# Layer 3's output tiles: odd tiles stored through ScalarE's DMA queue instead of GpSimd's, and the general path's stores off GpSimd's queue too

## The chip, the cores and the metric

One Trainium2 chip, one of its cores. The metric is device time in microseconds (us) of one execution, the median of a few runs. Engines are named as in the profile: PE (TensorE), DVE (VectorE), ACT (ScalarE), POOL (GpSimd) and SP (SyncE, which here only issues DMAs).

## What is computed

Four graph layers on 2708 nodes with 256 features, each followed by a residual and a layer norm. The adjacency matrix is dense in storage. Cut to what matters here:

```
x = LN(x + adj @ (x * w0))                         # layer 0
x = LN(x + attention(x, adj > 0))                  # layer 1, 4 heads
x = LN(x + signed_attention_and_GRUs(x, adj))      # layer 2, 3 heads, uses adj > 0 and adj < 0
h = adj @ (x @ neigh_W.T) / (adj.sum(1) + 1)       # layer 3
x = LN(x + concat(x, h) @ lin_W.T)
```

The output has 2708 rows of 256 floats: 22 tiles of 128 rows, the last of 20.

## The kernel before

**The main path.** The kernel streams the adjacency matrix from HBM again in every layer and multiplies tiles of it on PE. In layers 2 and 3 the nodes are cut into two halves and each half into three units of 512, 512 and 330 columns; a seven-product scheme (`seven`, L309) forms the products, with the operand sums on DVE (L296 to L299). The last part of the program is layer 3: for each of the three units, eleven chunks of the matrix are loaded into three rotating buffers `p` by SP (`load_pairs`, L256), one chunk feeding 14 matmul records of L309.

**Finishing rows.** What a unit has accumulated is gathered (L317 to L327: one copy on ACT, four adds on DVE), and then a generator, `rows3`, finishes one row tile at a time: two transposes on PE (L1172), a scaled add on DVE (L1173), the moments on DVE (L162 to L166) with the power -1/2 on POOL (L167), one small multiply on DVE (L1177), the normalization on ACT (L1178), and the store of the tile to the output (L1179). Rows of unit 0 (tiles 0 to 3 and 11 to 13) are finished between the matmuls of unit 1, those of unit 1 (4 to 7 and 14 to 17) between the matmuls of unit 2, and those of unit 2 (8 to 10 and 18 to 21) after the last matmul, at the end of the program: `between()` takes one step of the generators after products 2 and 5 of each chunk. Even tiles are stored through SP's queue, odd ones through POOL's.

**The order of work.** Each engine takes its instructions in the order in which the program was built; an engine's DMAs wait in that same order. A framework adds the semaphores: each DMA takes one of eight semaphores of its kind in turn (one set of eight for SP's and ACT's DMAs together, one for POOL's), and a DMA waits until the one that had its semaphore before it has landed.

**The general path.** Layers 2 and 3 in the main path are valid for a matrix without negative entries. A flag `signed` is computed in layer 1, and at the end of the program stands a branch (L1425): where the flag is set, `layer2_signed()` and `layer3()` compute both layers again. With the inputs here it isn't set, and the body is skipped. Two stores to DRAM stand in that body: `layer2_end` (L219, 22 stores of `y3_d`) and `layer3` (L1225, 22 stores of the output). On the skipping side of the branch the framework puts instructions that bring each semaphore to the count that it would have had after the body, so that what follows can wait for one number whichever side ran. For the semaphores of SP's, ACT's and the engines' own these are single semaphore updates; for those of POOL's DMAs it is one POOL instruction that the trace calls INC_SWDGE_SEM. After it, under L1468 (the end of the program's context), SP waits for all semaphores, every engine executes a DRAIN and they meet in a barrier; POOL is the one that collects the others and releases them, and then clears the semaphores.

Of the kernel before, what the change touches and what calls it, by code (L numbers as in the profile page):

```python
# [19 lines left out]
P = 128  # L20
# [7 lines left out]
def kernel(  # L28
# [24 lines left out]
    nc = tc.nc  # L53
# [27 lines left out]
    def sz(i):  # L81
        return min(P, N - i * P)
# [19 lines left out]
    def pool(name, bufs=1, **kw):  # L102
        return tc.tile_pool(name=name, bufs=bufs, reuse_waits="tile", **kw)
# [34 lines left out]
    y3_d = [dram.tile([sz(t), F], F32, name=f"y3_{t}") for t in range(NT)]  # L138
# [20 lines left out]
    def moments(src, n):  # L159

        bst = small.tile([P, 6], F32, tag="bn_st", name="bn_st")
        nc.vector.bn_stats(bst[:n], src[:n])  # L162
        mv = small.tile([P, 2], F32, tag="bn_mv", name="bn_mv", bufs=12)
        nc.vector.bn_aggr(mv[:n], bst[:n])
        rstd = small.tile([P, 1], F32, tag="bn_rs", name="bn_rs", bufs=12)
        nc.vector.tensor_scalar(rstd[:n], mv[:n, 1:2], EPS, None, ALU.add)  # L166
        nc.gpsimd.tensor_tensor(rstd[:n], rstd[:n], neg_half[:n], ALU.pow)  # L167
        return mv[:n, 0:1], rstd[:n]

    def layernorm(dst, src, n):  # L170

        mean, rs = moments(src, n)
        nc.vector.tensor_scalar(dst[:n], src[:n], mean, rs, ALU.subtract, ALU.mult)

    def transposed(ps, pool, src, n, tag):

        pt = ps.tile([P, 4, P], F32, tag="tr", name="tr")
        for f in range(FC):
            nc.tensor.transpose(pt[:, f, :n], src[:n, f * P : (f + 1) * P], ident[:n, :n])
        dst = pool.tile([P, FC, P], F32, tag=tag, name=tag)  # L180
        nc.scalar.copy(dst[:, :, :n], pt[:, :FC, :n])
        return dst
# [9 lines left out]
    def load_strip(pool, t):  # L192
        s = pool.tile([P, NT, P], F32, tag="strip", name="strip", bufs=2)
        nc.sync.dma_start(s, adj_t[t])
        return s
# [5 lines left out]
    def strip_matmul(acc, s, n, rhs):  # L201
        for c in range(NT):
            nc.tensor.matmul(acc, s[:, c, :n], rhs(c), start=(c == 0), stop=(c == NT - 1))  # L203
# [6 lines left out]
    def layer2_end(ps, pool, lwn, t, y):  # L210

        n = sz(t)
        xt = transposed(ps, pool, y, n, "xt")
        pz = ps.tile([P, 2 * F], F32, tag="pz", name="pz")
        for f in range(FC):
            nc.tensor.matmul(pz[:n], xt[:, f, :n], lwn[:, f, :], start=(f == 0), stop=(f == FC - 1))
        nc.scalar.copy(h3[t][:n], pz[:n, F:])
        nc.vector.tensor_tensor(y[:n], y[:n], pz[:n, :F], ALU.add)
        nc.gpsimd.dma_start(y3_d[t], y[:n])  # L219

    def gru_columns(pool, b, bih, bhh):

# [90 lines left out]
    def gathered(pool, m, w, wide, tag, bufs=1):  # L313

        m1, m26, m75, m43 = m
        m1s = pool.tile([P, wide], F32, tag="m1s", name="m1s", bufs=2)
        nc.scalar.copy(m1s[:, :w], m1[:, :w])  # L317
        y = pool.tile([P, FC, 2, wide], F32, tag=tag, name=tag, bufs=bufs)
        yq = y.rearrange("p f h w -> p (f h) w")[:, :, :w]
        nc.vector.tensor_tensor(  # L320
            yq[:, 0::3], m1s[:, None, :w].to_broadcast([P, 2, w]), m26[:, :, :w], ALU.add
        )
        nc.vector.tensor_tensor(
            yq[:, 1:3], yq[:, 3:4].to_broadcast([P, 2, w]), m75[:, :, :w], ALU.add
        )
        nc.vector.tensor_tensor(yq[:, 3], yq[:, 1], m75[:, 1, :w], ALU.add)
        return y, nc.vector.tensor_tensor(yq[:, 1:3], yq[:, 1:3], m43[:, :, :w], ALU.add)  # L327
# [57 lines left out]
    if True:  # L385
# [13 lines left out]
        if True:  # L399
# [162 lines left out]
            if True:  # L562
# [276 lines left out]
                for lo in range(0, NT, 4):  # L839
# [3 lines left out]
                    for t in range(lo, hi):  # L843
                        n = sz(t)
# [80 lines left out]
    with (  # L925
# [10 lines left out]
        def bank():  # L936
            return banks.tile([P, W], F32, tag="bank", name="bank")
# [132 lines left out]
        def by_tiles(lo, w, src, ends):  # L1070

            tiles, at = [], 0
            for t, c0, c1 in pieces(lo, w):
                got = src(at, c1 - c0)
                at += c1 - c0
                if c1 - c0 < sz(t):
                    first = t not in ends
                    if first:
                        ends[t] = nleft.tile([P, FC, P], F32, tag=f"yt{t}", name=f"yt{t}")
                    nc.gpsimd.tensor_copy(ends[t][:, :, c0:c1], got)  # L1080
                    if first:
                        continue
                    got = ends[t]
                tiles.append((t, got))
            return tiles
# [40 lines left out]
        for u, (_, w) in enumerate(units):  # L1126
            est = [nleft.tile([P, FC, W], F32, tag="est", name="est", bufs=3) for h in range(2)]
            for k in range(K):
# [23 lines left out]
                y, summed = gathered(nleft, m, w, W, "yk")  # L1152
# [6 lines left out]
        def complete(u):  # L1159

            return [t for t in by_end if ends_at[t] == u]

        def rows3(u, y, o8):

            a, w = units[u]
            for h in range(2):
                for t, src in by_tiles(h * NH + a, w, lambda at, n: y[:, :, h, at : at + n], shared3):
                    n = sz(t)
                    o = o8[:, complete(u).index(t)]
                    pt = bank()  # L1170
                    for f in range(FC):
                        nc.tensor.transpose(pt[:n, f * P : (f + 1) * P], src[:, f, :n], ident)  # L1172
                    nc.vector.scalar_tensor_tensor(  # L1173
                        o[:n], pt[:n, :F], rdeg[:n, t : t + 1], o[:n], ALU.mult, ALU.add
                    )
                    mean, rs = moments(o, n)
                    nc.vector.scalar_tensor_tensor(mean, mean, -1.0, rs, ALU.mult, ALU.mult)  # L1177
                    nc.scalar.activation(o[:n], o[:n], AF.Identity, scale=rs, bias=mean)  # L1178
                    (nc.gpsimd if t % 2 else nc.sync).dma_start(out[t * P : t * P + n, :], o[:n])  # L1179
                    yield  # L1180


# [2 lines left out]
        for u, (_, w) in enumerate(units):  # L1185
            m = accumulators()
            for i, c in enumerate(lead):
                early3 = u == 0 and max(ends_at[2 * c], ends_at[2 * c + 1]) + 1 < len(units)
                if u == 0:
                    if not early3:  # L1190
                        while urgent or later:
                            between()
                    hq[c] = quarter_sums(xqp, h3, c, "hq")
                pa = nright.tile([P, 2, 2, W], F32, tag="p", name="p", bufs=3)
                load_pairs(units, u, c, pa)
                if i == MH - 3:
                    o8 = (nleft if u % 2 else hold).tile([P, 4 * W // F, F], F32, tag="blk", name="o8")
                    for j, t in enumerate(complete(u)):
                        nc.gpsimd.dma_start(o8[: sz(t), j], y3_d[t])
                with tc.issue_after(summed.ins):  # L1200
                    seven(nright, m, pa, h3, hq[c], c, w, i == 0, i == MH - 1, range(7) if early3 else (2, 5))
            y, summed = gathered(nleft, m, w, W, "yk")
            later.append(rows3(u, y, o8))
# [8 lines left out]
    def layer3():  # L1212
        with pool("l3", 2, side="right") as l3, pool("ps_3", 3, space=PSUM) as ps_3:
            for t in range(NT):
                n = sz(t)
                s = load_strip(l3, t)
                o = l3.tile([P, F], F32, tag="o", name="o")
                nc.sync.dma_start(o[:n], y3_d[t])
                acc = ps_3.tile([P, 512], F32, tag="acc", name="acc")
                strip_matmul(acc[:n, :F], s, n, lambda c: h3[c])  # L1220
                nc.vector.scalar_tensor_tensor(
                    o[:n], acc[:n, :F], rdeg[:n, t : t + 1], o[:n], ALU.mult, ALU.add
                )
                layernorm(o, o, n)
                nc.gpsimd.dma_start(out[t * P : t * P + n, :], o[:n])  # L1225

    def layer2_signed():
        TG = 4
# [127 lines left out]
        with tc.tile_pool(name="l2b", bufs=1) as l2b:  # L1356
# [5 lines left out]
            for t in range(NT):  # L1362
# [56 lines left out]
                )  # L1419
                layernorm(y, y, n)  # L1420
                layer2_end(ps_t, work, lwn, t, y)
        stack.close()


    with tc.If(nc.values_load(signed[0:1, 0:1], min_val=0, max_val=1) > 0):  # L1425
        layer2_signed()
        layer3()
# [44 lines left out]
```

## Time and profile before

| | us |
|---|---|
| median of 3 runs | 1934.03 |
| lowest and highest run | 1933.43, 1934.38 |
| the profiled execution, its own time | 1935.28 |
| its span, first to last instruction | 1933.5 |
| PE busy in the span | 1866.2 |
| DVE, ACT, POOL busy | 1316.4, 617.7, 269.6 |

The profile is one execution on the chip, and times in it count from the first instruction. A busy engine is one with an instruction of its datapath under way; semaphore updates, branches and drains are not counted as busy, but the lists of one source line show them, with a q behind the engine's name (POOLq). In such a list a row reads: line, engine, operation, count, shortest/median/longest duration in ns, and when the first and the last of them started. DMAs that POOL issues run in the queue that the profile calls software_dynamic, those of SP and ACT in two hardware_dynamic ones.

The store of one full tile is 128 KB. In the profile, 11 stores of L1179 are issued by SP (median 357 ns each) and 11 by POOL (median 576 ns each); from issue to landing they took 1.7 to 4.3 us.

### The profile page before, as it was taken

How to read it: one execution, taken by the hardware profiler on the slowest of the kernel's cores; microseconds unless marked ns; L12 is line 12 of the kernel's file. 1: busy time of each engine (PE TensorE's matmuls, PEld its weight loads, DVE VectorE, ACT ScalarE, POOL GpSimd, SP SyncE). 2: the span in 40 equal slices, each digit the busy share in tenths (PEclk: the TensorE clock that was granted, in tenths of full speed). 3: DMA queues.
4: the chain of work that ended last, by engine and by line, in shares of the span. 5: the costliest groups of instructions: out<-in, count | busy, mean ns of one | idle time of the engine just before them, and what ended most of it. 6: DMA issues, size and time to landing. Idle time of an engine off the chain costs nothing.

```text
span 1933.5 us, 22594 instructions
## 1 busy us (share of the span) xinstructions
PE 1866.2 (97%) x7475; PEld 1012.0 (52%) x7479; DVE 1316.4 (68%) x2409; ACT 617.7 (32%) x1064; POOL 269.6 (14%) x446
## 2 busy tenths in 40 slices
PE   8999989999999999999899999999999999999995
PEld 6888832222233778778444444444445555554453
DVE  4344369899898947455567888586877758745664
ACT  4444400000100103111345655555554555311010
POOL 1212110001112421000001000110200201211211
PEclk9999989999999999999999999999999999999997
DMA  8344400000000647555746656453554445633753
GB/s 291 125 142 164 150 23 1 1 29 9 15 1 23 161 105 192 143 134 116 210 133 184 190 154 179 122 162 97 164 156 111 128 102 134 178 110 108 199 154 84
DMA packets 431964, 235.90 MB, mean 122 GB/s; under 512 B 172162, under 2 KB 419332, under 8 KB 429406
## 3 DMA queue, kind: packets, MB, share of 16 engines
q1 hardware_dynamic: 416158, 207.40, 39.1%
q0 software_dynamic: 8272, 22.53, 3.7%
q10 hardware_dynamic: 7408, 4.43, 0.8%
q8 instruction: 62, 1.02, 0.2%
q14 instruction: 64, 0.52, 0.1%
HBM read 221.61 MB, written 12.65 MB: 121 GB/s over the span
## 4 chain that ended last, share of the span: by engine, by line
PE 80%; DMA 6%; DVE 6%; issue 2%; ACT 2%; SPq 1%; POOL 1%; DVEq 0%; POOLq 0%; ACTq 0%
PE m L309 38%; PE acc L647 10%; PE acc L203 7%; PE bank L1007 7%; PE den L656 5%; PE gate L882 4%; PE bank L983 3%; DMA strip<-in_adj_t_dram 2%; DVE p L665 2%; PE bank L1058 2%; SPq L256 1%; ACT below L452 1%; PE pm L410 1%; DVE p L1141 1%; POOL bn_rs L167 1%
## 5 line engine op out<-in xcount | busy, mean ns | idle before, releaser
L665 DVE SCALAR_TENSOR_TENSOR p<-fall_b,rise,mask 128x1024 f32<-128x1024 f32 (+1 forms) x264 | 297.9, 1150 | 27.7 <-PE den L656 15.2
L1137 ACT ACTIVATE p<-st,e_neg 128x1024 f32<-128x1024 f32 (+1 forms) x198 | 197.2, 1041 | 206.7 <-PE m L309 202.6
L309 PE MATMUL m<-s,xq 128*128 128x512 f32 (+3 forms) x660 | 230.1, 467 | 0.0
L647 PE MATMUL acc<-p,h 128*64 128x512 f32 (+2 forms) x1056 | 224.3, 557 | 3.0 <-DVE p L665 2.8
L203 PE MATMUL acc<-turn,strip 128*128 128x257 f32 (+1 forms) x836 | 191.6, 380 | 0.0
L309 PE MATMUL m<-p,xq 128*128 128x512 f32 (+1 forms) x396 | 183.1, 544 | 0.7 <-DVE yk L327 0.4
L1140 ACT ACTIVATE p<-p 128x1024 f32<-128x1024 f32 (+1 forms) x198 | 179.0, 944 | 0.2
L309 PE MATMUL m<-p,x 128*128 128x512 f32 (+1 forms) x396 | 169.7, 547 | 5.1 <-DVE p L1141 4.8
L1141 DVE TENSOR_TENSOR p<-p,blk 128x1024 f32<-128x1024 f32 (+1 forms) x132 | 142.6, 1099 | 41.9 <-ACT p L1140 28.0
L203 PEld LDWEIGHTS acc<-turn,strip 128*128 128x128 f32 (+1 forms) x836 | 151.5, 185 | 25.3 <-issue 0.5
L296 DVE TENSOR_TENSOR s<-p 128x512 f32<-128x512 f32 (+1 forms) x132 | 83.0, 630 | 119.6 <-PE m L309 105.2
L309 PEld LDWEIGHTS m<-s,xq 128*128 128x128 f32 x660 | 124.3, 190 | 74.6 <-issue 57.9
L647 PEld LDWEIGHTS acc<-p,h 128*64 128x64 f32 x1056 | 65.4, 136 | 147.8 <-issue 117.7
L167 POOL TENSOR_TENSOR bn_rs<-bn_rs,neg_half 128x1 f32<-128x1 f32 (+1 forms) x110 | 82.8, 754 | 371.4 <-DVE bn_rs L166 364.2
L309 PE MATMUL m<-s,x 128*128 128x512 f32 (+3 forms) x330 | 127.1, 467 | 0.0
L656 PE MATMUL den<-p,h 128*32 128x512 f32 (+2 forms) x1056 | 124.4, 553 | 2.8 <-DVE p L665 2.7
L309 PEld LDWEIGHTS m<-p,x 128*128 128x128 f32 x396 | 74.9, 191 | 79.2 <-issue 61.1
L309 PEld LDWEIGHTS m<-p,xq 128*128 128x128 f32 x396 | 74.5, 190 | 78.1 <-issue 61.2
L452 ACT ACTIVATE below<-strip 128x384 bf16<-128x384 f32 x132 | 78.6, 595 | 72.4 <-DMA strip<-in_adj_t_dram 69.0
L681 ACT COPY den<-den 64x512 f32<-64x512 f32 (+2 forms) x12 | 6.4, 530 | 249.8 <-PE den L656 249.7
L1141 DVE TENSOR_TENSOR p<-p,turn 128x1024 f32<-128x1024 f32 (+1 forms) x66 | 71.6, 1106 | 20.7 <-ACT p L1140 12.6
L299 DVE TENSOR_TENSOR s<-p,s 128x512 f32<-128x512 f32 (+1 forms) x132 | 83.6, 633 | 2.0
(244 smaller groups left out, 2526.2 us busy)
## 6 DMA issues: line engine op xcount, KB each, us to landing
strip<-in_adj_t_dram SPq DMA_DIRECT2D x19, 1408.0 KB, 6.1
blk<-in_adj_t_dram SPq DMA_DIRECT2D x88, 256.0 KB, 3.4
blk<-in_adj_t_dram SPq DMA_DIRECT2D x88, 192.0 KB, 4.1
pa<-in_adj_t_dram SPq DMA_DIRECT2D x110, 128.0 KB, 2.7
turn<-in_adj_t_dram SPq DMA_DIRECT2D x44, 256.0 KB, 3.1
blk<-in_adj_t_dram SPq DMA_DIRECT2D x88, 128.0 KB, 2.5
p<-in_adj_t_dram SPq DMA_DIRECT2D x44, 256.0 KB, 3.5
turn<-in_adj_t_dram SPq DMA_DIRECT2D x44, 192.0 KB, 3.2
```

The lines of the kernel that those rows point to most:

```text
L167: nc.gpsimd.tensor_tensor(rstd[:n], rstd[:n], neg_half[:n], ALU.pow)
L203: nc.tensor.matmul(acc, s[:, c, :n], rhs(c), start=(c == 0), stop=(c == NT - 1))
L299: nc.vector.tensor_tensor(s4, a12, s2, ALU.subtract)
L309: nc.tensor.matmul(dst[:, :w], lt, rt, start=start and not (one_bank and i), stop=stop and not (one_bank and i in (1, 2, 5)))
L452: nc.scalar.activation(below[:, : (hi - lo) * P], s[:, lo:hi].rearrange("p c n -> p (c n)"), AF.Relu, scale=-1.0, accum_out=negative[:, BE ...
L647: nc.tensor.matmul(acc[s][i * HD : (i + 1) * HD, :ws], hs[c][:, 2 * q + i, :HD], ps[i][:, p0 : p0 + ws], **flags,)
L656: nc.tensor.matmul(den[j : j + CT, :ws], hs[c][:, 2 * q + i, HD + 1 - CT :], ps[i][:, p0 : p0 + ws], **flags,)
L665: nc.vector.scalar_tensor_tensor(p[:, :w], falls[g // 2][:, 2 * q + i, :w], rise[:, c, 2 * q + i : 2 * q + i + 1], mask[:, c, at : at + w] ...
L1007: nc.tensor.matmul(g[:, :w], lt, rt, start=(q == 0), stop=(q == len(terms) - 1))
L1137: nc.scalar.activation(p[:, :, :w], st_k[:, :, :w], AF.Relu, scale=-1.0, bias=e_neg[:, at, k : k + 1])
L1140: nc.scalar.activation(p[:, :, :w], p[:, :, :w], AF.Exp, scale=-1.0)
L1141: nc.vector.tensor_tensor(p[:, :, :w], p[:, :, :w], blk[:, i, :, :w], ALU.mult)
```

## The change

Three lines name another queue. Nothing that is computed changes, no working instruction of PE or DVE is added, removed or put in another place, and the tiles stored are the same.

```diff
         nc.vector.tensor_tensor(y[:n], y[:n], pz[:n, :F], ALU.add)
-        nc.gpsimd.dma_start(y3_d[t], y[:n])
+        nc.scalar.dma_start(y3_d[t], y[:n])
...
                     nc.scalar.activation(o[:n], o[:n], AF.Identity, scale=rs, bias=mean)
-                    (nc.gpsimd if t % 2 else nc.sync).dma_start(out[t * P : t * P + n, :], o[:n])
+                    (nc.scalar if t % 2 else nc.sync).dma_start(out[t * P : t * P + n, :], o[:n])
                     yield
...
                 layernorm(o, o, n)
-                nc.gpsimd.dma_start(out[t * P : t * P + n, :], o[:n])
+                nc.sync.dma_start(out[t * P : t * P + n, :], o[:n])
```

The first hunk is `layer2_end` (called in the skipped body alone), the second `rows3` of the main path, the third `layer3` (skipped). In the built program this moves 11 stores from POOL's stream to ACT's in the main path, and 44 out of POOL's stream in the skipped body, 22 to ACT and 22 to SP. POOL keeps its other DMAs in the main path, the last of which are the loads of L1199. On the skipping side of the branch POOL's part goes from seven instructions (an update, four waits, INC_SWDGE_SEM and a branch) to two, the update and the branch; INC_SWDGE_SEM is no longer there. The list of what SP waits for at the end has the same length.

## The prediction

> **What bounds the kernel now.** I read the page's busy times first, then the chain of waits, then the end of the program line by line, because the change touches nothing before the last 7% of the span.
>
> ```profile
> PE 1866.2 (97%) x7475; PEld 1012.0 (52%) x7479; DVE 1316.4 (68%) x2409; ACT 617.7 (32%) x1064; POOL 269.6 (14%) x446
> ```
>
> PE holds the whole program, so a queue change can pay only where PE has stopped. The table of stretches for layer 3 shows where (stretch, length, then busy us and count by engine):
>
> ```profile
> 1798.00:1810.00 12.00, 12.00 (x35) 5.59 (x34) 10.25 (x30) 1.80 (x3) 3.19 (x5) 1.00 0.62 175
> ...
> 1862.00:1880.00 18.00, 16.05 (x62) 9.79 (x61) 15.46 (x51) 3.60 (x6) 5.79 (x10) 1.00 0.58 155
> 1880.00:1908.00 28.00, 27.87 (x102) 19.09 (x102) 15.02 (x37) 1.64 (x3) 2.52 (x4) 1.00 0.57 144
> 1908.00:1922.00 14.00, 3.28 (x16) 2.26 (x14) 9.60 (x39) 4.09 (x7) 5.73 (x12) 0.61 0.16 50
> ```
>
> While the rows of unit 0 are finished (first line) PE is full; while those of unit 1 are (second line) it loses 2 us; from 1908 PE is done. The chain, cut to the end, stops early:
>
> ```profile
> 1920.58 0.58 POOL out_dram L1179
> 1921.15 0.55 issue
> 1921.70 0.54 POOLq L1425
> ```
>
> It ends at 1922.2, and the span at 1933.5: 11.3 us follow that no busy instruction fills. The lists of the two lines that own them, L1425 (branch and catching up) and L1468 (the end):
>
> ```profile
> L1425 SPq EVENT_SEMAPHORE  x8: 17/17/17, 1924.6 to 1925.1; - x8
> L1425 SPq COMPARE_BRANCH  x1: 53/53/53, 1921.3 to 1921.3; - x1
> L1425 ACTq COMPARE_BRANCH  x1: 54/54/54, 1921.4 to 1921.4; - x1
> L1425 POOLq TENSOR_LOAD <-signed x1: 811/811/811, 1921.7 to 1921.7; - x1
> L1425 POOLq COMPARE_BRANCH  x1: 50/50/50, 1922.6 to 1922.6; - x1
> L1425 ACTq EVENT_SEMAPHORE  x1: 17/17/17, 1924.4 to 1924.4; - x1
> L1425 POOLq INC_SWDGE_SEM  x1: 1471/1471/1471, 1925.8 to 1925.8; - x1
> ```
>
> ```profile
> L1468 SPq EVENT_SEMAPHORE  x12: 28/28/28, 1927.3 to 1928.0; - x12
> L1468 SPq DRAIN  x2: 7/10/13, 1928.0 to 1928.1; - x2
> L1468 POOLq DRAIN  x1: 5291/5291/5291, 1927.4 to 1927.4; - x1
> ```
>
> Every engine loses about 3 us between its branch and its next instruction (SP 1921.3 to 1924.6, ACT 1921.4 to 1924.4). Then POOL alone sets the end: INC_SWDGE_SEM 1925.8 to 1927.3, a DRAIN 1927.4 to 1932.6, then the barrier, 0.9 us. The others are done by 1928.1; SP itself stood from 1925.1 to 1927.3 for what INC_SWDGE_SEM sets.
>
> **What the Trainium skill says.** (1) "Perfetto Trace Analysis", section "Sequencer-only Instruction (DRAIN, etc)": the window shown is execution, and the wait for semaphores isn't in it. So the 5.29 us are no wait for a stated semaphore but for work still in POOL; the trace agrees in that POOL's three other drains took 0.05 to 0.18 us. (2) The same page, "DMA Instruction — SWDGE (GPSIMD)": the end shown for a DMA that POOL issues is the last descriptor written, and the cores complete the instruction later. That lets unseen work stand behind a POOL record; no run here shows it yet. (3) "DMA: Bandwidth & Descriptors", section "Issuing engines are not separate DMA queues": all queues run on the same 16 engines, another queue saves only issue time. The trace agrees roughly: landing 2.0 us by SP, 3.1 by POOL at the medians. (4) "Runtime: NRT & Kernel Launch", section "Instruction fetch mechanics": a taken branch out of the fetched window waits for a fetch; that fits the 3 us seen on every engine, which the change leaves.
>
> **The change, part by part.**
>
> *Skipped stores (L219, L1225).* 44 stores that don't run cost nothing; what they leave is the catching up. INC_SWDGE_SEM goes (1.47 us and four waits before it, 1925.4 to 1925.8); the SP and ACT sums only grow in value: eight updates by SP, as before, 0. Saved on POOL's path: 1927.3 - 1925.4 = 1.9 us.
>
> *POOL's last stores.* In the tail POOL's stream ended with the stores of tiles 19 and 21, the second held until ACT finished (1921.4); its flag load came at 1921.7 and its branch at 1922.6. After, its last work is the power of tile 21, 1920.1 to 1920.6 in the timeline, so its flag load (0.81) starts between 1919.9 and 1920.6 and its branch stands at 1920.8 to 1921.5: 1.1 to 1.8 us earlier. Plus the same 2.8 us (1922.6 to 1925.4), POOL is at its DRAIN at 1923.7 to 1924.4, 3.0 to 3.7 us before the old 1927.4. The 2.8 may shrink, as POOL's skipped body falls from 286 to 200 instructions; I count nothing for it and keep it for a rival.
>
> *The DRAIN.* The disputed term. Ends: 0.05 us (its shortest neighbour) and 5.29 us (unchanged). Which depends on what it flushes. The last POOL stores had landed by 1924.3 (their semaphore's counts) and INC_SWDGE_SEM's wait for them had passed, so no store is in flight at 1927.4. What immediately precedes is INC_SWDGE_SEM; at the program's start a DRAIN behind small POOL work took 0.18. I take 0.2: the 5.29 are the tail of INC_SWDGE_SEM or of stores issued 6 us earlier, and after the change neither exists; POOL's last DMA is then the load of L1199 at 1827.9, 96 us before.
>
> *ACT gets 11 stores.* Price 0.35 us each to issue, from ACT's own 128-partition stores at L355 (median 349 ns): 3.8 us. Eight fall in 1798 to 1908 where PE's matmuls cover them; ACT is busy 5.2 of 46 us from 1862 to 1908. Queued behind them is the next L1178, whose result only a store awaits, and once per unit the copy L317, not near one. Without that cover each costs at most 0.35. In the tail the store of tile 19 is issued under the activation of tile 20 (1920.3 to 1920.9): 0. Tile 21's waits for the last activation, 1921.4, then 0.35, flag load 0.48, branch at about 1922.4, 3.0 us to the next instruction: ACT is through at 1925.5 instead of 1924.5. SP's last wait counts on it.
>
> *SP's new neighbours.* ACT's stores take semaphores from SP's set of eight, so a load of L256 eight DMAs later waits for an ACT store to land. In unit 2 SP has little to spare: seven loads of 0.47 (0.51 apart) are 3.6 us a chunk against 14 matmuls, 3.9. But SP's own even store, between the two, already waits for a later activation: tile 5's (the first odd one) activation ends at 1870.2 and its store should land by 1872.5 (2.0 to 2.4), before SP passes the next even store at 1873.7. Tightest is the last, tile 17: activation done 1884.9, landed about 1887.3, wanted by the ninth DMA after 1883.1, at 1887.7. I take 0, bounds -1 (a 1.46 us issue at 1876.2, beside a POOL store, may go) and +2.
>
> **Sum.** SP: branch unchanged, updates to 1925.2, then its end list and drain, 0.8 (1927.3 to 1928.1): ready at 1926.1. ACT 1925.5, POOL 1924.6. So SP decides; POOL then needs 1933.5 - 1932.6 = 0.9. Span 1926.9 to 1927.0, 6.5 less than 1933.5. The profiled execution of 1935.28 (1.8 around its span) becomes 1928.8; it stood 1.25 above the median of 1934.03, so the median becomes 1934.03 - 6.5 = 1927.5. What is late next: SP, and the 3 us behind its branch.
>
> **Rivals.**
> 1. *Forecast: the DRAIN shrinks.* 1927.5; own range 1926.5 (-1) to 1929.5 (+2). For: nothing in flight, short drains elsewhere. Against: no run shows a drain without INC_SWDGE_SEM late in the program.
> 2. *The DRAIN keeps its 5.3 us* because it pays for all of POOL's DMAs since the start, of which dozens remain. It only starts 3.0 to 3.7 earlier: 1930.3 to 1931.0, say 1930.7. If POOL's branch became near as well (2.8 less), it would end at 1926.6, and the time would be 1928.5.
> 3. *Slower: SP's loads stand behind ACT's stores.* Place: L256 while unit 0's and 1's rows are finished. Price: at most one landing, 2.0 us, for each of eight stores, 16 us, less 6.5: 1943.5. It decides once the stall exceeds 6.5 + 3.9 = 10.4 us, 1.3 a store. Against: the stores land before SP's next even store passes, and PE is full through unit 1.
> 4. *No change: the end is held by something the drain only hides,* such as ACT's later arrival with a longer fetch, or the change doing nothing to POOL: 1934. Against: INC_SWDGE_SEM is gone from the built program, and the others' readiness at 1928.1 is in the trace.
>
> **Chances.** 1: 0.58, 2: 0.28, 3: 0.06, 4: 0.08. 0.2%, 3.9 us, is about what a measurement of this kernel can tell from no change: faster means below 1930.2. That takes case 1 nearly whole (0.57) and the short end of 2 (0.05): 0.62; same, the rest of 2, of 1 and case 4: 0.32; slower 0.06. The range runs from case 1's lower end to case 2's upper with some spread, 1926.5 to 1931.5, and leaves out 3 and 4.
>
> **What would show it.** Right: no INC_SWDGE_SEM at L1425, POOL's DRAIN at L1468 under 0.3 us, starting near 1924, SP's last drain at about 1926.1 and the end 0.9 later; PE's busy time and the stretches to 1908 unchanged within 1 us. Wrong: a DRAIN of 5 us that merely starts earlier (case 2), or PE idle growing from 1862 to 1880 with L256 waiting for stores of `out_dram` (case 3).

## The result, and the profile after

| | before | after |
|---|---|---|
| median of 20 runs, us | 1932.88 | 1928.94 |
| lowest and highest run | 1930.6, 1935.71 | 1926.4, 1932.88 |
| the profiled execution | 1935.28 | 1929.04 |
| its span | 1933.5 | 1927.3 |
| last activation of L1178 ends, in the span | 1921.4 | 1920.4 |
| tail: from there to the end of the span | 12.06 | 6.83 |

The ratio is 0.998, with a 95% interval of 0.9974 to 0.9986: 3.9 us faster (2.7 to 5.0). Executions of one kernel differ by several us, as the table shows. Over the eleven traces of this study the last activation of L1178 ends between 1916.3 and 1921.4 us, but the time from the start of the first of these activations to that point stays within 120.4 to 121.0 us: the difference comes from work long before the change's place. So what follows measures from the end of the last activation, which all kernels have. Against that point, the profiled execution gained 5.2 us. L1178 before, then after:

```profile
L1178 ACT ACTIVATE o<-o,bn_mv,bn_rs x22: 586/601/602, 1800.9 to 1920.8; 128x256 f32<-128x256 f32 x21, 20x256 f32<-20x256 f32 x1
```

```profile
L1178 ACT ACTIVATE o<-o,bn_mv,bn_rs x22: 585/600/602, 1799.4 to 1919.8; 128x256 f32<-128x256 f32 x21, 20x256 f32<-20x256 f32 x1
```

The busy times of the page after: DVE as before, PE 2.2 us less (within what executions differ by), POOL with its eleven stores fewer, ACT no busier (the issue of a DMA by ACT isn't counted).

```profile
PE 1864.0 (97%) x7475; PEld 1011.5 (52%) x7479; DVE 1316.4 (68%) x2409; ACT 617.2 (32%) x1064; POOL 261.2 (14%) x435
```

The table of stretches after (stretch, length, then busy us and count by engine):

```profile
1798.00:1810.00 12.00, 12.00 (x37) 5.79 (x36) 10.24 (x30) 2.40 (x4) 2.58 (x4) 1.00 0.75 208
...
1862.00:1880.00 18.00, 16.18 (x65) 9.98 (x64) 14.84 (x52) 3.60 (x6) 4.30 (x8) 1.00 0.57 151
1880.00:1908.00 28.00, 27.58 (x100) 18.57 (x98) 14.96 (x35) 1.63 (x3) 1.36 (x2) 1.00 0.55 138
1908.00:1922.00 14.00, 1.68 (x13) 1.30 (x13) 8.67 (x38) 4.09 (x7) 4.32 (x9) 0.77 0.21 64
```

PE's busy time in the three stretches up to 1908 is 12.00, 16.18 and 27.58 us, against 12.00, 16.05 and 27.87 before. Between them, from 1845 to 1862, it is 16.21 against 17.00: PE's wait for a load of `p`, 0.69 us from 1862.0 before, is 0.79 us from 1860.5 after and so falls into the earlier stretch. No cost of ACT's stores to the matmuls shows; from the first to the last activation of L1178 it took 120.5 us before and 121.0 after, so half a microsecond isn't excluded. The stores themselves, L1179 after:

```profile
L1179 SPq DMA_DIRECT2D out_dram<-o x11: 333/356/612, 1800.1 to 1920.0; - x11
L1179 ACTq DMA_DIRECT2D out_dram<-o x11: 338/338/552, 1803.2 to 1920.5; - x11
```

An odd store takes 338 ns of ACT instead of 576 ns of POOL. All that is left is the end. The branch and what follows it, L1425 after:

```profile
L1425 SPq EVENT_SEMAPHORE  x8: 17/17/17, 1923.4 to 1923.9; - x8
...
L1425 POOLq TENSOR_LOAD <-signed x1: 487/487/487, 1918.8 to 1918.8; - x1
L1425 POOLq COMPARE_BRANCH  x1: 50/50/50, 1919.4 to 1919.4; - x1
...
L1425 SPq COMPARE_BRANCH  x1: 53/53/53, 1920.3 to 1920.3; - x1
...
L1425 ACTq COMPARE_BRANCH  x1: 58/58/58, 1921.7 to 1921.7; - x1
L1425 POOLq EVENT_SEMAPHORE  x1: 17/17/17, 1921.9 to 1921.9; - x1
...
L1425 ACTq EVENT_SEMAPHORE  x1: 17/17/17, 1924.3 to 1924.3; - x1
```

INC_SWDGE_SEM, POOL's catching up, is gone. POOL takes its branch at 1919.4, a microsecond before the last activation ends (before: a microsecond after it). The end of the program's context, L1468 after:

```profile
L1468 SPq EVENT_SEMAPHORE  x14: 17/28/28, 1924.0 to 1927.2; - x14
...
L1468 POOLq DRAIN  x3: 50/106/4392, 1922.0 to 1927.0; - x3
L1468 SPq DRAIN  x3: 7/7/13, 1924.7 to 1926.7; - x3
```

Before, SP waited for INC_SWDGE_SEM until 1927.3; now it goes through its list without a stop (1924.0 to 1924.7). But POOL's DRAIN is still there: 4.392 us, 1922.0 to 1926.4, and the end follows 0.8 us later. The forecast had 0.2 us for it. So the path of the end still runs through POOL, and the question for the experiments is what this DRAIN pays for.

### The profile page after: what moved, and what is told of

Its sections match the earlier page's. It is cut to its first block, busy times and chain, and to the rows that moved or that the text cites. A ratio compares the mean times of both kernels' runs of the same rounds, so it can differ in the third digit from the quotient of the medians.

```text
span 1927.3 us, 22585 instructions
## 1 busy us (share of the span) xinstructions
PE 1864.0 (97%) x7475; PEld 1011.5 (52%) x7479; DVE 1316.4 (68%) x2409; ACT 617.2 (32%) x1064; POOL 261.2 (14%) x435
## 4 chain that ended last, share of the span: by engine, by line
PE 80%; DMA 6%; DVE 6%; ACT 3%; issue 2%; SPq 2%; POOL 1%; ACTq 0%; DVEq 0%; POOLq 0%
PE m L309 38%; PE acc L647 10%; PE acc L203 7%; PE bank L1007 7%; PE den L656 5%; PE gate L882 4%; PE bank L983 3%; DMA strip<-in_adj_t_dram 2%; DVE p L665 2%; PE bank L1058 2%; SPq L256 1%; ACT below L452 1%; DVE p L1141 1%; PE pm L410 1%; POOL bn_rs L167 1%
## 5 line engine op out<-in xcount | busy, mean ns | idle before, releaser
L167 POOL TENSOR_TENSOR bn_rs<-bn_rs,neg_half 128x1 f32<-128x1 f32 (+1 forms) x110 | 81.8, 745 | 380.1 <-DVE bn_rs L166 373.2
L297 DVE TENSOR_TENSOR p<-p 128x512 f32<-128x512 f32 (+1 forms) x132 | 83.0, 629 | 1.7
```

## The experiments

Theory D, for debt: the DRAIN pays a fixed price for each DMA that POOL has issued and not settled since, however long ago it landed. Rivals: N, nearness: it is the tail of stores issued shortly before; I: it is the tail of INC_SWDGE_SEM, or comes with it; F: it costs the same whatever POOL did. A DMA is called *settled* here when no DRAIN pays for it any more; that is a name for what the lengths show, as no record shows the settling. All "before" runs beside the experiments have medians of 1932.45 (e1 to e4) and 1932.7 (e5 to e8). Times with a plus sign count from the end of the last activation.

### e1 and e2: each half alone

e1 is the kernel before with only the store of the main path moved:

```diff
-                    (nc.gpsimd if t % 2 else nc.sync).dma_start(out[t * P : t * P + n, :], o[:n])
+                    (nc.scalar if t % 2 else nc.sync).dma_start(out[t * P : t * P + n, :], o[:n])
```

> Only the 11 stores of L1179 move to ACT; the skipped body keeps POOL's stores, so INC_SWDGE_SEM stays. Counted from the end of the last activation of L1178 (in before POOL's DRAIN starts 5.9 us after it and the program ends 12.1 after it; in the changed kernel 1.6 and 6.8). Debt theory (POOL's last DRAIN pays for the software DMAs that POOL issued since its last DRAIN): INC_SWDGE_SEM about 2.2 to 3.7 us after the activation, DRAIN 4.4 us or a little more behind it, end at 8.9 to 9.8, so 2.3 to 3.2 us faster than before. INC theory (the 0.9 us by which the DRAIN was longer before belong to INC_SWDGE_SEM): DRAIN 5.3, end at 9.8. If the 0.9 belong to the late stores: DRAIN 4.4, end at 8.9.

Measured: 1929.26 (ratio 0.9983, 0.9975 to 0.9991), tail 9.21 us. Behind the branch of e1, and at its end:

```profile
L1425 POOLq COMPARE_BRANCH  x1: 50/50/50, 1918.9 to 1918.9; - x1
...
L1425 POOLq INC_SWDGE_SEM  x1: 1251/1251/1251, 1922.4 to 1922.4; - x1
```

```profile
L1468 POOLq DRAIN  x3: 46/106/4392, 1923.6 to 1928.6; - x3
```

INC_SWDGE_SEM is still there, 1.251 us where it took 1.471, directly ahead of a DRAIN (1923.6) of exactly the length of after. The kernel after, without it, has the same DRAIN, so the DRAIN doesn't come from it: theory I falls.

e2 is the kernel before with only the skipped stores moved:

```diff
-        nc.gpsimd.dma_start(y3_d[t], y[:n])
+        nc.scalar.dma_start(y3_d[t], y[:n])
...
-                nc.gpsimd.dma_start(out[t * P : t * P + n, :], o[:n])
+                nc.sync.dma_start(out[t * P : t * P + n, :], o[:n])
```

> Only the stores of the skipped body move; the odd tiles of L1179 are still stored by POOL, INC_SWDGE_SEM is gone. From the end of the last activation: POOL's branch as before at about 1.2 us, DRAIN from 4.1. If the 0.9 us longer DRAIN of before belongs to the late stores: DRAIN 5.3, end at 10.2 (1.9 us faster than before). If it belongs to INC_SWDGE_SEM: DRAIN 4.4, end at 9.4 (2.7 us faster).

Measured: 1931.63 (0.9992, 0.9985 to 0.9999), tail 10.25 us. The DRAIN in e2:

```profile
L1468 POOLq DRAIN  x3: 50/106/5291, 1924.0 to 1929.9; - x3
```

No INC_SWDGE_SEM, and the DRAIN takes 5.291 us as before. The tails give the halves: the stores 2.85 us, the skipped stores 1.81, the change as a whole 5.23 of 12.06. The 0.6 us that the halves lack lie in what varies without the change: the fetch behind POOL's branch (2.99 us in e1, 2.59 in after) and the barrier of the end (0.3 us longer in e1).

### e3 and e4: a DRAIN put where POOL is idle

e3 is the kernel after with one more DRAIN on POOL, behind the last loads of L1199 at 1822 us, when PE has some 80 us of matmuls ahead. e4 is the same edit in the kernel before, where the DRAIN starts at 1825.

```diff
-                        nc.gpsimd.dma_start(o8[: sz(t), j], y3_d[t])
+                        got = nc.gpsimd.dma_start(o8[: sz(t), j], y3_d[t])
+                    if u + 1 == len(units):
+                        with tc.issue_after(got.ins):
+                            nc.gpsimd.drain()
```

> The changed kernel with one more DRAIN on POOL right behind its last DMAs (the loads of L1199 for unit 2, at about 1828), where POOL has nothing to do for 30 us. Debt theory: the early DRAIN takes 4 us or more under PE's matmuls, the last one falls to 0.2 us or less; SP then ends the program 4.4 + 0.9 = 5.3 us after the last activation, 1.5 us faster than the changed kernel. Fixed-price theory (a late DRAIN on POOL costs 4.4 us whatever came before): the last DRAIN stays at 4.4 and the time is that of the changed kernel.

> The kernel before with the same early DRAIN; INC_SWDGE_SEM and three POOL stores still come after it. Debt theory: the last DRAIN falls to 0.1 to 1 us, the program ends 6.9 to 7.7 us after the last activation, 4.4 to 5.2 us faster than before. INC theory in its strong form (the DRAIN is the tail of INC_SWDGE_SEM) and fixed-price theory: DRAIN 5.3, time as before.

Measured: e3 1925.21 (0.9956, 0.9941 to 0.9972), tail 4.89 us; e4 1927.3 (0.9969, 0.9959 to 0.9979), tail 6.26. The end of e3:

```profile
L1471 POOLq DRAIN  x3: 38/47/106, 1919.1 to 1922.1; - x3
L1471 SPq DRAIN  x3: 7/7/13, 1921.5 to 1921.8; - x3
```

and the DRAIN that was added:

```profile
L1202 POOLq DRAIN  x1: 9093/9093/9093, 1821.9 to 1821.9; - x1
```

The DRAIN at the end, the one at 1919.1, is 0.047 us: the debt was paid at 1822, where it cost 9.1 us of POOL and nothing of PE, which stays full:

```profile
1810.00:1833.00 23.00, 23.00 (x56) 10.30 (x55) 12.27 (x24) 1.20 (x2) 5.18 (x9) 1.00 0.77 217
```

F falls, as the same instruction at the same place now costs next to nothing, and POOL's other work isn't charged: 15 powers of L167 and four copies lie between the two DRAINs. e4 keeps the late stores and INC_SWDGE_SEM:

```profile
L1428 POOLq INC_SWDGE_SEM  x1: 332/332/332, 1923.7 to 1923.7; - x1
```

```profile
L1471 POOLq DRAIN  x3: 46/106/626, 1924.1 to 1925.3; - x3
```

With seven stores behind the added DRAIN, three of them after the last matmul, the DRAIN of the end takes 0.626 us, not 5.3: N falls as the main part. INC_SWDGE_SEM shrank from 1.471 to 0.332 us too, so it grows with the same debt at a lower rate; it pays nothing off, as the DRAIN behind it in e1 is as long as without it.

### e5 and e6: how the debt is counted

e5 is the kernel after with the DRAIN behind the stores of L855 at 749 us (75 POOL DMAs follow it), e6 with the DRAIN of e3 one unit earlier, behind the loads of L1199 at 1665 us (18 follow it).

```diff
-                                nc.gpsimd.dma_start(st_d[u][:, h, off : off + c1 - c0], sr[:, c0 - at : c1 - at])
+                                got = nc.gpsimd.dma_start(st_d[u][:, h, off : off + c1 - c0], sr[:, c0 - at : c1 - at])
+                with tc.issue_after(got.ins):
+                    nc.gpsimd.drain()
```

```diff
-                    if u + 1 == len(units):
+                    if u == 1:
```

> The changed kernel with one more DRAIN on POOL behind the stores of L855, at the end of layer 1: 59 of POOL's 134 software DMAs lie before it, 75 after it. If the debt is proportional to the DMAs since the last DRAIN, the last DRAIN takes 75/134 of 4.39, 2.5 us (end about 1.9 us before the changed kernel's). If it grows with the last few dozen alone (a full ring), it stays at 4.39 and so does the time.

> The same with the DRAIN behind the loads of L1199 for unit 1, after which POOL issues 18 more DMAs. Proportional: 18/134 of 4.39, 0.6 us, and SP becomes the one that ends the program, as with the DRAIN behind the last load. Full ring: between 0.6 and 4.39. The added DRAIN stands in front of loads of L238 and of POOL's part of finishing rows: if that is not covered by PE, the stretch before the tail grows by up to 4 us.

Measured: e5 1928.37 (0.9976, 0.9963 to 0.9989), tail 8.96 us, longer than the 6.83 of after, because its last DRAIN is longer:

```profile
L1470 POOLq DRAIN  x3: 50/106/6182, 1918.2 to 1925.0; - x3
```

The medians (1928.37 of six runs, 1928.94 after) don't tell the two apart. e6 1925.43 (0.9949, 0.9932 to 0.9965), tail 4.97, with this end:

```profile
L1471 POOLq DRAIN  x3: 50/106/1527, 1921.1 to 1924.1; - x3
```

With 0, 7, 18 and 75 DMAs since the added DRAIN, the last one took 0.047, 0.626, 1.527 and 6.182 us. From the first to the last that is 6.135 / 75 = 0.0818 us for each DMA, and the two between lie on the line: 0.05 + 7 x 0.0817 = 0.62, 0.05 + 18 x 0.0817 = 1.52. Some of these DMAs were issued over a millisecond before. For e5 both expectations missed: in proportion to all 134 DMAs it would have been 2.5 us, with the last few dozen alone 4.39. The same proportion gave 0.6 for e6. The price is 0.08 us for a DMA, not 4.39 / 134 = 0.03, and so only 53 were owed at the end of the kernel after.

The line is that of the DRAINs at the end, which start when POOL's DMAs have landed. A DRAIN right behind DMAs can take longer. That of e5 took 7.1 us, 0.5 of it for the last store still being written, and all 59 DMAs before it are worth only 0.05 + 59 x 0.0817 = 4.87. In e3, writing the two loads queued ahead took 1.25 us of the 9.09, and the 53 DMAs that the kernel after owes at its end are worth 4.38; 3.5 us remain. The loads in front of it took 3.2 to 6.5 us to land, so it may have waited for them, but no run separates that.

### e7 and e8: which stores, or how many

e7 leaves the eight odd tiles of units 0 and 1 on POOL and moves only the three of the tail to ACT, e8 the other way round (edits of the line after).

```diff
-                    (nc.scalar if t % 2 else nc.sync).dma_start(out[t * P : t * P + n, :], o[:n])
+                    ((nc.gpsimd if u < 2 else nc.scalar) if t % 2 else nc.sync).dma_start(out[t * P : t * P + n, :], o[:n])
```

```diff
-                    (nc.scalar if t % 2 else nc.sync).dma_start(out[t * P : t * P + n, :], o[:n])
+                    ((nc.gpsimd if u == 2 else nc.scalar) if t % 2 else nc.sync).dma_start(out[t * P : t * P + n, :], o[:n])
```

> The changed kernel with the eight odd tiles of units 0 and 1 stored by POOL again and the three odd tiles of the tail by ACT. If the 0.9 us by which the DRAIN is longer before (5.29 against 4.39) are the price of the number of stores, the DRAIN takes 4.39 + 8/11 of 0.9, 5.0 us; if they are the price of stores shortly before the end, 4.39.

> The other half: the three odd tiles of the tail stored by POOL, the eight of units 0 and 1 by ACT. By number: DRAIN 4.39 + 3/11 of 0.9, 4.6 us; by nearness: 5.29. POOL's branch comes about 2.2 us later than in the changed kernel, since it waits for the last activation and issues the store; the end 2.3 (number) to 3.1 us (nearness) later than the changed kernel's.

Measured: e7 1928.66 (0.998, 0.9972 to 0.9989), tail 7.48; e8 1929.76 (0.9984, 0.9975 to 0.9993), tail 9.56. The DRAIN of e7, then that of e8:

```profile
L1468 POOLq DRAIN  x3: 50/106/5046, 1918.7 to 1924.4; - x3
```

```profile
L1468 POOLq DRAIN  x3: 50/106/4637, 1922.0 to 1927.2; - x3
```

Eight early stores add 5.046 - 4.392 = 0.654 us, three late ones 4.637 - 4.392 = 0.245, eleven 5.291 - 4.392 = 0.899: 0.0817 us each in all three. When they were issued makes no difference to the DRAIN, and neither does their size: the eight early ones move 1024 KB and the three late ones 276 KB (tile 21 has 20 rows), so in proportion to bytes the three would have added 0.18 us, not 0.245. What the three late ones do besides is hold up POOL's branch. L1425 of e7, then of e8:

```profile
L1425 POOLq TENSOR_LOAD <-signed x1: 494/494/494, 1915.5 to 1915.5; - x1
L1425 POOLq COMPARE_BRANCH  x1: 50/50/50, 1916.1 to 1916.1; - x1
...
L1425 SPq COMPARE_BRANCH  x1: 53/53/53, 1917.1 to 1917.1; - x1
```

```profile
L1425 SPq COMPARE_BRANCH  x1: 53/53/53, 1917.9 to 1917.9; - x1
...
L1425 POOLq TENSOR_LOAD <-signed x1: 838/838/838, 1918.2 to 1918.2; - x1
L1425 POOLq COMPARE_BRANCH  x1: 50/50/50, 1919.1 to 1919.1; - x1
```

POOL takes its branch 1.0 us ahead of SP in e7 and 1.2 us behind it in e8: 2.2 us, and the larger part of the stores' gain.

### e9: what settled the first 81

The kernels without an added DRAIN don't fit the whole count. The kernel after issues 134 DMAs on POOL and its DRAIN pays for (4.392 - 0.05) / 0.0817 = 53; the kernel before issues 145 and pays for 64. In both, 81 are missing. e9 is the kernel after with a DRAIN behind POOL's 28th DMA, at 261 us.

```diff
-                nc.gpsimd.dma_start(fall_d[:, t * P : t * P + n], turned[:, :n])
+                got = nc.gpsimd.dma_start(fall_d[:, t * P : t * P + n], turned[:, :n])
+                if t == NT - 1:
+                    with tc.issue_after(got.ins):
+                        nc.gpsimd.drain()
```

> The kernel after with one DRAIN on POOL behind its 28th DMA (the last small store of the first layer, about 262 us); 106 POOL DMAs follow it. The last DRAIN so far costs 0.05 us + 0.0817 us for each DMA still owed, but without an added DRAIN the number owed is the total less 81 (134 gave 53, 145 gave 64), and with a DRAIN 75 DMAs from the end all 75 were owed. Theory A (POOL settles by itself whenever about 81 are owed): 106 - 81 = 25 owed, last DRAIN about 2.1 us. Theory B (a certain place in the program, between the 81st and 82nd DMA at 1365 us, settles everything): 53 owed as in the kernel after, 4.39 us. Theory C (nothing but a DRAIN settles, and the first 81 were cheap for another reason): 106 owed, 8.7 us.

Measured, in one run: 1926.34, before 1933.78 beside it; tail 5.33 us. The DRAIN that was added, and its last one:

```profile
L430 POOLq DRAIN  x1: 2909/2909/2909, 260.9 to 260.9; - x1
```

```profile
L1471 POOLq DRAIN  x3: 50/106/2916, 1920.8 to 1924.3; - x3
```

The first pays for 28 DMAs, 0.05 + 28 x 0.0817 = 2.34 us; most of the rest, 0.57, is the 28th still being written when it starts (0.52 us). The last: (2.916 - 0.05) / 0.0817 = 35 of the 106 DMAs that followed: 71 were settled on the way. So B (a fixed place, 53) and C (nothing but a DRAIN, 106) are wrong, and A only has it right that some are settled without a DRAIN; its number isn't 81 each time: 81 from the start of the program, 71 from e9's DRAIN, and in e5 none of 75. These counts are worked out from the DRAINs' lengths. No instruction in the trace shows the settling. Which DMAs are settled, whether at once, and what decides the time (a ring of descriptors that fills would be one candidate) stays open.

### The tails against the medians

| kernel | POOL DMAs | last DRAIN, us | DMAs it paid for, at 0.0817 us | tail, us | tail less that of before | median less its before |
|---|---|---|---|---|---|---|
| before | 145 | 5.291 | 64 | 12.06 | | |
| after | 134 | 4.392 | 53 | 6.83 | -5.2 | -3.9 |
| e1, stores only | 134 | 4.392 | 53 | 9.21 | -2.9 | -3.2 |
| e2, skipped only | 145 | 5.291 | 64 | 10.25 | -1.8 | -0.8 |
| e3, after + DRAIN | 134 | 0.047 | 0 | 4.89 | -7.2 | -7.2 |
| e4, before + DRAIN | 145 | 0.626 | 7 | 6.26 | -5.8 | -5.2 |
| e5, DRAIN at 749 | 134 | 6.182 | 75 | 8.96 | -3.1 | -4.3 |
| e6, DRAIN at 1665 | 134 | 1.527 | 18 | 4.97 | -7.1 | -7.3 |
| e7, late stores moved | 142 | 5.046 | 61 | 7.48 | -4.6 | -4.0 |
| e8, early stores moved | 137 | 4.637 | 56 | 9.56 | -2.5 | -2.9 |

Each tail is that of one execution, and the DRAIN came out the same to the nanosecond in both pairs of kernels that owe the same. The two last columns agree within 1.3 us, about what the medians' intervals leave. So to that precision the tail accounts for the times, and no work before it needs to be called on. e3 and e6 are faster than both kernels of this study, at 0.9956 and 0.9949 of before.

## Why the prediction fell within its range although its main term failed

It said 1927.5 and a gain of 6.5 us; the median is 1928.94, within the range, and the gain 3.9 (2.7 to 5.0), 5.2 in the profiled tail. That it lies within the range is in part luck: the range reached over the first two rivals and could not tell them apart, and an error of 4.2 us in its main term came to 1.3 us in the tail. POOL's DRAIN started 1.4 us earlier than the sum had it (+1.6, not +3.0), and 1.5 us of what was left were covered by SP, which the sum had ready that much behind POOL.

*The step that failed: "The DRAIN."* The prediction put: "I take 0.2: the 5.29 are the tail of INC_SWDGE_SEM or of stores issued 6 us earlier, and after the change neither exists". It took 4.392. Its premise, that nothing is in flight, was true and didn't matter: the price is for each DMA issued and not settled, although it has landed, and 53 of them were left. What happened is nearest to the second rival, which paid "for all of POOL's DMAs since the start, of which dozens remain"; that one overrated the debt (81 were no longer owed) and gave it no rate, so it kept 5.3 us where eleven DMAs less make 0.9 less. The prediction's point (1), that the window of such an instruction holds no wait for semaphores, was no safe ground either: here the measurement differs, and some windows do hold one, such as that of a semaphore instruction of ACT under L1178 before, 8.592 us from 1905.3 to the activation of 1914.0. For the DRAIN it is the length, which follows the count of DMAs, that speaks against such a wait. The kernels with the debt paid early test the rest of the sum: e3 is 7.2 us under before, in the tail as in the median, where the forecast with a DRAIN of 0.2 us had 6.5.

*The skipped stores, 1.9 us: right.* From POOL's first instruction behind the branch to its DRAIN it took 1.9 us before and 0.08 after; e2 alone shortens the tail by 1.81.

*POOL's branch, 1.1 to 1.8 us earlier: 2.2.* Against the last activation it moved from +1.15 to -1.07. Two things were missed. The flag load doesn't wait for POOL's last work: it starts at 1918.8, and the last power of L167 runs at 1919.1 beside it. And it took 0.487 us where 0.811 was assumed: in before, e2, e4 and e8, where POOL is writing its last store at the same time, it took 0.811 to 0.845, and in the seven others 0.487 to 0.496. The step behind the branch, counted at "the same 2.8", took 2.6. Together the DRAIN starts 4.3 us earlier (+5.92 to +1.60), where 3.0 to 3.7 were forecast. The sum of the tail is then 4.3 + 0.9 = 5.2.

*What is late next: SP, as forecast, but behind POOL.* SP's last drain was forecast for 1926.1, which is +4.7; it came at +4.39, and in e3 at +4.08, where it does set the end 0.8 us later. ACT was forecast through at 1925.5, +4.1; it was at +4.0.

*ACT's stores at 0, SP's loads at 0: right within half a microsecond.* 338 ns each; the stores of both queues landed in 1.7 to 4.0 us (2.3 at the median), and in the list of who waited for L1179 one activation, 2.0 us in all; PE's stretches as shown above. The slower rival's stalls don't show. The fourth, no change, is outside the interval.

*What a POOL record leaves out.* The prediction took from the Trainium skill, "Perfetto Trace Analysis", section "DMA Instruction — SWDGE (GPSIMD)", that work can stand behind the record of a DMA that POOL issues, and no run showed it. Now the runs do, but not as I read it: what the last DRAIN pays for isn't the completion of recent DMAs but a charge for every one that is owed, however old, 0.082 us each.

## What to carry to other kernels

A long DRAIN on POOL at the end of a program is a bill for the software DMAs behind it: two traces with different numbers of them give the price of one (the whole count overstates the bill: here 81 of 134 weren't on it). Either issue them by another engine, or put a DRAIN on POOL behind its last DMA, where it is idle and nothing waits for it. Being landed doesn't settle a DMA, so "nothing in flight" is no reason to price a DRAIN at nothing. To see gains of a few us in a program of 1930, measure the tail from an instruction that both kernels have, and let the medians confirm it.

## What the runs showed of the hardware beyond that

- A DRAIN on POOL took 0.05 us with nothing owed, and 0.0817 us more for each unsettled POOL DMA, on the line for 7, 18 and 75 DMAs, and with the same step for 3, 8 and 11 more, whatever their bytes; right behind a DMA it took more in e5, 6.6 us where 59 DMAs are worth 4.87. INC_SWDGE_SEM took 1.471, 1.251 and 0.332 us with 64, 53 and 7 owed, about 0.02 us for each.
- By the DRAINs' lengths, POOL settles some of its DMAs by itself without a record in the trace: 81 in before and after, 71 in e9, none of 75 in e5. A DRAIN too early can so make the last one longer: 6.182 us in e5 against 4.392.
- A flag load on POOL runs while POOL's datapath is at work and takes 0.49 us; with a software DMA of POOL's being written it took 0.81 to 0.85 (0.825 in e2 and 0.838 in e8, 0.494 in e7).
